# A two-layer graph network on one core: block 0 of x and the line weight loaded as squares of 32 and turned by VectorE

## The chip, the cores and the metric

The kernel runs on one NeuronCore of a Trainium2 chip. The metric is device time in microseconds (us) of one execution: the median of three runs is 1557.29 (1557.27 to 1557.6). Times inside the execution are counted in us from the start of the profiled span.

## The reference

Two layers over 4096 nodes with 512 channels and a dense 4096 x 4096 adjacency of 0 and 1. Cut to what matters:

```python
# layer 0
Ab   = A > 0
keep = Ab & (cumsum(Ab, axis=1) <= 64)            # the first 64 neighbours of each row
cnt  = keep.sum(axis=1, keepdims=True)
xj   = leaky_relu((keep @ X) / max(cnt, 1) @ W_nb.T + b_nb)
xi   = leaky_relu(X @ W_line.T + b_line)
x    = layernorm(X + xi + where(cnt > 0, xj, 0))
# layer 1: attention of one head over the same adjacency
Wh   = x @ W + bW
e    = leaky_relu_0.2((Wh @ a1 + b1)[:, None] + (Wh @ a2 + b2)[None, :])
att  = softmax(where(adj > 0, e, -9e15), axis=1)
x    = layernorm(x + att @ Wh)
```

The change touches the first 25 us of layer 0: the first products `X @ W_nb.T` and `X @ W_line.T`. The kernel takes `X @ W_nb.T` before the sum over neighbours, so that each block of x meets both weights.

## The kernel before, in words

x is cut into 32 blocks of 128 rows. A product on TensorE contracts over the partitions, so a block of x is wanted turned (`xt`, channels on the partitions), and so are both weights (`wt_nb`, `wt_line`). There are two ways to turn a 128 x 512 piece:

- **By TensorE** (`turn_by_pe`, L319): VectorE rearranges the piece into tile `t` (`squares`, L313), TensorE turns four 128 x 128 parts by transposes (L156), and ScalarE (or VectorE, for one piece) copies the bank out of PSUM (L157).
- **By VectorE** (`turn_x`, L332): the piece is loaded by four DMAs of 64 KB, one for each group of 32 partitions, in runs of 512 bytes (`load_turned_x`, L301), so that one VectorE transpose of 32 x 32 squares over the whole tile finishes it.

Before, block 0 (loaded whole into `xb` by `load_own_x`, L308) and all eight pieces of the two weights (`load_w`, L358) go by TensorE; blocks 1 and up go by VectorE, through three buffers `late` (tiles `c`), so that block i + 3 can be loaded once block i is turned.

The order of the work is written out by hand: each engine takes its instructions in the order of the program text, and every engine that issues DMAs (SP, ACT and POOL here) has a queue of its own. A DMA signals its end on one of eight semaphores for the loads of SP and ACT together, and one of another eight for POOL's, taken in turn; an issue that gets a semaphore in use waits for the DMA that holds it.

The start (L438 to L465 of the code) runs so. SP loads block 0, two pieces of nb, block 1 in squares, two pieces of line, and the line bias; ACT loads the other two pieces of nb and two of line. TensorE runs 15 transposes of the identity (`spin`, L364), which warm its clock. Then come the turn of block 0 and of pieces 0 to 2 of nb; the product of block 0 with the first three quarters of nb (L381, width 384), with the turn of piece 3 behind its first matmul; two line pieces; the last quarter (width 128); the other two line pieces; the turn of block 1; block 1 times nb (`pys[1]`), block 0 times line (`pls[0]`). Blocks 2 and 3 are issued on POOL, each behind a small VectorE memset into its buffer (L448), which holds them back until VectorE gets there. The weight of layer 1 (`raw["w"]`), rows of a1, a2 and the bias, and the first two pieces of the adjacency follow on SP behind another memset (L458).

After that come the turn of block 2 (`turn_pair(1, 0)`), differences of the two weights (L517, L518), the two parts of y for blocks 0 and 1 (L431, L432), the turn of block 3 into the buffer that block 0 leaves, the line bias of block 0 (L416), block 1 times line, three sums over blocks 2 and 3 (L502 to L504), and the bias of block 1. ScalarE bends the result (L420) and writes the bias into a bank (L608); then a loop `seven(g)` (products at L511) takes two blocks at a time by a scheme with seven half products in place of eight, and encodes the adjacency beside it.

A line number in the profile is that of the instruction in the source; a helper has one line for all that call it.

Of the kernel before, what the change touches and what calls it, by code (L numbers as in the profile page):

```python
# [9 lines left out]
F32 = mybir.dt.float32  # L10
# [3 lines left out]
I32 = mybir.dt.int32  # L14
# [6 lines left out]
P = 128  # L21
SQ = 32
# [10 lines left out]
def two_layer_adj_gnn(  # L33
# [16 lines left out]
    nc = tc.nc  # L50
    N, C = x.shape
    NB = N // P
    NC = C // P
    NT = NB // 2
    CH = 2048
# [52 lines left out]
    late = [rows.tile([P, C], F32, name="c") for _ in range(3)]  # L108
# [28 lines left out]
    with ExitStack() as l0:  # L137
        adj_p = l0.enter_context(tc.tile_pool(name="l0_adj", bufs=2))
# [10 lines left out]
        def transpose_to(dst, src_of, n, wide, move):  # L149

            if wide:
                pt = ps_acc.tile([P, n, P], F32, name="acc")
            else:
                pt = ps_s.tile([P, n, P], F32, name="pt")
            for k in range(n):
                nc.tensor.transpose(pt[:, k, :], src_of(k), ident)  # L156
            move(dst, pt)  # L157
# [128 lines left out]
        with ExitStack() as la:  # L286
            work = la.enter_context(tc.tile_pool(name="l0_work", bufs=2))
            wp = la.enter_context(tc.tile_pool(name="l0_w", bufs=1))
# [3 lines left out]
            w_t = {}  # L292
            xrs, xbs, xts, pys, pls = {}, {}, {}, {}, {}
            lines = {}

            def load_turned_x(i, queue=nc.gpsimd):

                if i < NB:
                    xrs[i] = late[i % 3].rearrange("p (j c) -> p j c", c=P)
                    for n in range(NC):  # L300
                        queue.dma_start(  # L301
                            xrs[i][ts(n, SQ)],
                            x_blk(i)[:, ts(n, P)].rearrange("(j a) c -> a j c", a=SQ),
                        )

            def load_own_x(i, queue):
                xbs[i] = work.tile([P, C], F32, name="xb", bufs=1)
                queue.dma_start(xbs[i], x_blk(i))  # L308

            def squares(src):  # L310

                t = work.tile([P, C], F32, name="t", bufs=4)
                nc.vector.tensor_copy(  # L313
                    t.rearrange("p (m n b) -> p m n b", m=NC, b=SQ),
                    src.rearrange("p (n m b) -> p m n b", m=NC, b=SQ),
                )
                return t

            def turn_by_pe(dst, src, t=None, wide=False, move=nc.scalar.copy):  # L319
                t = squares(src) if t is None else t  # L320
                transpose_to(dst, lambda m: t[:, ts(m, P)], NC, wide, move)

            def xt_tile():
                return work.tile([P, NC, P], F32, name="xt", bufs=3)

            def turn_x(i, t=None):
                if i < NB:
                    xts[i] = xt_tile() if t is None else t
                    if i == 0:
                        turn_by_pe(xts[i], xbs[i])  # L330
                    else:
                        nc.vector.transpose(  # L332
                            xts[i].rearrange("p m (j a) -> p j m a", a=SQ),
                            xrs.pop(i).rearrange("p j (m b) -> p j m b", b=SQ),
                        )


            def early(name):
                dt = I32 if name == "a" else BF16
                t = adj_p.tile([P, CH], dt, name=name).bitcast(F32)  # L340
                return t.rearrange("p (c q) -> p c q", q=C)

            raw = {}
            for name in ("nb", "line"):
                t = early("a")
                raw[name] = [t[:, c, :] for c in range(NC)]
            raw["w"] = []
            for k in range(2):
                t = early("left")
# [3 lines left out]
            t = early("edge")  # L353
            early_rows += [t[:, c, :] for c in range(NC // 2)]

            def load_w(name, src, queues):
                for c in range(NC):
                    queues[c % len(queues)].dma_start(raw[name][c], src[ts(c, P), :])  # L358

            def spin(n):  # L360

                idle = ps_acc.tile([P, P], F32, name="acc")
                for _ in range(n):
                    nc.tensor.transpose(idle, ident, ident)  # L364

            def turn_w(name, parts=range(NC)):

                if name not in w_t:
                    w_t[name] = wp.tile([P, NC, C], F32, name=f"wt_{name}")
                moved = [squares(raw[name][c]) for c in parts]  # L370
                for c, t in zip(parts, moved):
                    turn_by_pe(
                        w_t[name][:, :, ts(c, P)], None, t, name == "nb",
                        nc.vector.tensor_copy if name == "nb" and c == 1 else nc.scalar.copy,
                    )

            def linear(lhs_t, name, bank=None, part=slice(0, C), behind_first=lambda: None):

                pl = ps_acc.tile([P, C], F32, name="acc") if bank is None else bank
                for k in range(NC):  # L380
                    nc.tensor.matmul(  # L381
                        pl[:, part], lhs_t[:, k, :], w_t[name][:, k, part],
                        start=(k == 0 and part.start == 0),
                        stop=(k == NC - 1 and part.stop == C),
                        skip_group_check=part.stop - part.start < C,
                    )
                    if k == 0:
                        behind_first()
                return pl
# [43 lines left out]
                    y_lo[i], src, y_hi[i].bitcast(F32), ALU.subtract  # L433
                )

            load_own_x(0, nc.sync)
            load_w("nb", w_nb, (nc.scalar, nc.sync))
            load_turned_x(1, nc.sync)  # L438
            load_w("line", w_line, (nc.scalar, nc.sync))
            nc.sync.dma_start(bias_line, b_line.partition_broadcast(P))  # L440
            spin(15)


            turn_x(0)
            turn_w("nb", range(3))

            for i in (2, 3):
                nc.vector.memset(late[i % 3][:, 0:1], 0.0)  # L448
                load_turned_x(i)
            pys[0] = linear(  # L450
                xts[0], "nb", part=slice(0, 3 * P), behind_first=lambda: turn_w("nb", range(3, 4))
            )
            turn_w("line", range(0, 2))
            linear(xts[0], "nb", pys[0], slice(3 * P, C))
            turn_w("line", range(2, 4))
            turn_x(1)
            load_turned_x(4)
            nc.vector.memset(raw["w"][0][:, 0:1], 0.0)  # L458
            load_w("w", w, (nc.sync,))
            load_rows(nc.sync)  # L460
            pys[1] = linear(xts[1], "nb")
            pls[0] = linear(xts.pop(0), "line")

            wide = [pls[0]]

# [29 lines left out]
            def turn_pair(g, r):  # L495
                i = 2 * g + r
                turn_x(i, (top, low)[r](g) if i < EDGE else None)
                load_turned_x(i + 3)
# [111 lines left out]
            for g in range(1, EDGE // 2):  # L610
                steps = idle
                q = done[0]
# [134 lines left out]
        for s in range(NB * NS):  # L747
            i, g = divmod(s, NS)
# [14 lines left out]
            for k in range(KB):  # L763
                j = g * KB + k
# [21 lines left out]
    wp = tile_p("l1_w", 3)  # L786
# [8 lines left out]
    early = wp.tile([P, NI, NS * SQ], F32, name="w")  # L795
# [460 lines left out]
    for q in range(NP * NT):  # L1256
# [6 lines left out]
        b = {2: 2 * g + 3, 3: 2 * g + 4}.get(k, 2 if q == 0 else NB)  # L1263
# [32 lines left out]
    p, rz = banks[NT - 1], rzs[NT - 1]  # L1296
# [62 lines left out]
```

## Time and profile before

| what | us |
|---|---|
| median of three timed runs | 1557.29 |
| lowest, highest | 1557.27, 1557.6 |
| span of the profiled execution, first to last instruction | 1555.1 |
| median less span | 2.19 |
| TensorE busy in the span | 1544.7 |
| TensorE, start of the first product (L381) | 7.79 |
| VectorE, start of the line bias of block 1 (L416) | 24.22 |
| TensorE, start of the product after it (L511) | 26.11 |

The profiled execution shows its span; its time by the device's clock is not listed apart from the three runs, so the span and the median stand side by side.

The profile is read as follows. PE is TensorE, DVE VectorE, ACT ScalarE, POOL GpSimd, SP SyncE; a name with q at its end is that engine's sequencer, which issues DMAs. A line of the timeline has the start, the length, the engine and line, the operation, the tile written and the tile read, the number of instructions merged, and in brackets the idle time before it and what ended it. A line of the waits has who waited, for whom, the total in us, how often, and the longest. A line of the chain has start, length and what the end of the program hung on there.

### The profile page before, as it was taken

What the parts mean: (1) busy time and instruction counts of PE and PEld (TensorE: products, weight loads), DVE (VectorE), ACT (ScalarE), POOL (GpSimd) and SP (SyncE); (2) the same over time, 40 slices, a digit from 0 to 9 for tenths busy, and PEclk for the clock granted to TensorE, in tenths of its full rate; (3) what the DMA queues carried; (4) which work ended last, traced back from release to release, by engine and by line L of the source; (5) the groups of instructions that cost most, each with busy time, mean ns of one, the idle gap of its engine ahead of it and who ended that gap; (6) DMA issues with size and microseconds to landing.
All of it is one profiled execution on the core that took longest, in us unless ns stands there. A gap on an engine that the chain in (4) does not pass through costs nothing.

```text
span 1555.1 us, 19124 instructions
## 1 busy us (share of the span) xinstructions
PE 1544.7 (99%) x6579; PEld 1241.5 (80%) x6579; DVE 1262.8 (81%) x2341; ACT 980.0 (63%) x1183; POOL 267.1 (17%) x424
## 2 busy tenths in 40 slices
PE   9999999999999999999999999999999999999998
PEld 5444468888888888878888888888888888888887
DVE  6988658989999998468888788887888888888864
ACT  3766558887888878427684577555775556755520
POOL 4544212212222122110001001111011110111101
PEclk9999999999999999999999999999999999999999
DMA  8965478879889887654122122221122211222202
GB/s 237 244 203 183 156 206 247 253 241 265 247 220 283 246 254 203 141 133 114 42 60 63 42 42 69 57 66 43 40 69 60 63 47 36 69 64 59 51 4 55
DMA packets 175425, 201.17 MB, mean 129 GB/s; under 512 B 102032, under 2 KB 135568, under 8 KB 167136
## 3 DMA queue, kind: packets, MB, share of 16 engines
q1 hardware_dynamic: 147472, 130.33, 29.7%
q0 software_dynamic: 26224, 67.64, 17.0%
q10 hardware_dynamic: 1632, 1.98, 0.4%
q8 instruction: 51, 0.84, 0.2%
q14 instruction: 46, 0.38, 0.1%
HBM read 141.03 MB, written 42.08 MB: 118 GB/s over the span
## 4 chain that ended last, share of the span: by engine, by line
PE 97%; DVE 1%; DMA 1%; ACT 0%; issue 0%; ACTq 0%; POOLq 0%; DVEq 0%; POOL 0%; SPq 0%
PE acc L1103 35%; PE acc L766 30%; PE pt L1103 14%; PE acc L511 9%; PE acc L917 4%; PE acc L381 3%; DMA w<-x_d 0%; PE pt L381 0%; DMA nat<-code_d 0%; DMA xb<-in_x_dram 0%; PE pt L156 0%; DVE c L849 0%; DMA st_d<-e 0%; PE acc L156 0%; DVE st L117 0%
## 5 line engine op out<-in xcount | busy, mean ns | idle before, releaser
L1103 PE MATMUL acc<-bt,s 128*128 128x256 f32 x1504 | 335.7, 379 | 0.0
L766 PE MATMUL acc<-y_hi,kt 128*128 128x512 f32 x824 | 320.5, 389 | 0.0
L766 PE MATMUL acc<-y_lo,kt 128*128 128x512 f32 x824 | 320.5, 389 | 0.0
L1103 PEld LDWEIGHTS acc<-bt,s 128*128 128x128 f32 x1504 | 285.8, 190 | 38.9
L988 ACT ACTIVATE w<-nat,few 128x1024 f32<-128x1024 uint8 x128 | 137.0, 1136 | 237.9 <-DVE a L1063 237.9
L1103 PE MATMUL acc<-bt,a 128*128 128x256 f32 x1056 | 239.0, 379 | 0.0
L1103 PE MATMUL pt<-bt,a 128*128 128x256 f32 x992 | 224.6, 379 | 0.0
L1103 PEld LDWEIGHTS acc<-bt,a 128*128 128x128 f32 x1056 | 200.6, 190 | 27.3
L1103 PEld LDWEIGHTS pt<-bt,a 128*128 128x128 f32 x992 | 188.5, 190 | 25.6
L280 ACT ACTIVATE kt<-ktb,few 128x1024 fp32r<-128x1024 uint8 x124 | 142.8, 1152 | 97.7 <-PE acc L766 80.1
L1063 DVE STREAM_TRANSPOSE a<-w 128x1024 f32<-128x1024 f32 x128 | 153.1, 1225 | 61.9 <-ACT w L1044 51.0
L126 POOL TENSOR_TENSOR rs<-ve,few 128x1 f32<-128x1 f32 x64 | 46.5, 727 | 807.6 <-DVE ve L124 800.2
L766 PEld LDWEIGHTS acc<-y_lo,kt 128*128 128x128 f32 x824 | 154.7, 188 | 32.2
L766 PEld LDWEIGHTS acc<-y_hi,kt 128*128 128x128 f32 x824 | 154.6, 188 | 32.1
L981 ACT ACTIVATE w<-w,st_n 128x1024 f32<-128x1024 f32 x128 | 149.3, 1232 | 16.1 <-DVE m L998 16.1
L1044 ACT ACTIVATE w<-w,nm 128x1024 f32<-128x1024 f32 x128 | 145.5, 1137 | 11.0 <-DVE nm L1035 11.0
L998 DVE CUSTOM_DVE_ANT_0 w<-e_n,w 128x1024 f32<-128x1024 f32 x128 | 149.5, 1220 | 1.3
L178 ACT ACTIVATE edge<-a,few 128x2048 bf16<-128x2048 int32 x64 | 136.2, 2129 | 4.6 <-issue 2.7
L226 ACT CAST code<-left 128x2048 uint8<-128x2048 bf16 x64 | 121.1, 1893 | 0.0
L209 DVE TENSOR_TENSOR left<-edge,left 128x2048 bf16<-128x2048 bf16 x64 | 78.4, 1225 | 2.2
L301 POOL DMA_DIRECT2D c<-in_x_dram x120 | 65.6, 554 | 64.0 <-DVE xt L332 45.1
L197 DVE TENSOR_TENSOR_SCAN left<-few,ends,left 128x1024 bf16<-128x1024 f32 x32 | 75.2, 2351 | 1.1
(229 smaller groups left out, 1999.4 us busy)
## 6 DMA issues: line engine op xcount, KB each, us to landing
a<-in_adj_dram SPq DMA_DIRECT2D x64, 1024.0 KB, 5.8
code_d<-code POOLq DMA_DIRECT2D x64, 256.0 KB, 4.0
nat<-code_d SPq DMA_DIRECT2D x248, 64.0 KB, 2.2
w<-x_d SPq DMA_DIRECT2D x128, 64.0 KB, 2.1
own<-in_x_dram SPq DMA_DIRECT2D x31, 256.0 KB, 3.2
own<-own_d POOLq DMA_DIRECT2D x31, 256.0 KB, 5.6
x_d<-own POOLq DMA_DIRECT2D x31, 256.0 KB, 4.7
c<-in_x_dram POOLq DMA_DIRECT2D x120, 64.0 KB, 5.0
```

The lines of the kernel that those rows point to most:

```text
L178: nc.scalar.activation(edge_of[s], loaded.pop(s).rearrange("p (t q) -> p q t", q=2), AF.Sigmoid, bias=steep[:, 0:1], scale=STEEP, accum_ou ...
L209: nc.vector.tensor_tensor(left, e, left, ALU.mult)
L226: nc.scalar.copy(code.bitcast(U8).rearrange("p (t q) -> p q t", q=2), seen_of.pop(s))
L280: nc.scalar.activation(kts[s], bytes_.rearrange("p t (i r) -> p t r i", r=2), AF.Sigmoid, bias=steep[:, 1:2], scale=STEEP,)
L511: nc.tensor.matmul(bank, lhs[:, k, :], rhs[:, k, :], start=start and k == 0, stop=k == 1, skip_group_check=True,)
L766: nc.tensor.matmul(accs[i], kt[:, k // 2, k % 2, :], term[j], start=(j == 0 and term is y_hi), stop=(j == NB - 1 and term is y_lo),)
L981: nc.scalar.activation(dst, src, AF.Prelu, bias=bias, scale=scale, alpha=0.2)
L988: nc.scalar.activation(wts[b][:, i, :], nats[b, i // 2].bitcast(U8)[:, i % 2, :], AF.Relu, bias=far, scale=-FAR,)
L998: nc.vector.tensor_tensor_reduce(w_i, e2_n, w_i, 1.0, -3e38, ALU.subtract, ALU.max, m4s[b][:, i : i + 1])
L1044: nc.scalar.activation(w_i, w_i, AF.Exp, bias=nms[b][:, i : i + 1], accum_out=z4s[g][:, r, i : i + 1])
L1063: nc.vector.transpose(a[:, r].rearrange("p s (i a) -> p i s a", a=SQ), wts[2 * g + r][:, :, ts(k, 8 * SQ)].rearrange("p i (s x) -> p i s x ...
L1103: nc.tensor.matmul(banks[g][n], lhs[:, j, :], bt[:, 4 * k + j, rhs, :], start=(k == 0 and j == 0 and n == mate[0]), stop=(k == NP - 1 and ...
```

## The change

Block 0 is loaded like every other block, by four DMAs of squares on SP, and turned by VectorE into `xt`. The line weight is no longer loaded by SP and ACT: sixteen DMAs of squares (four for each of its four pieces) go out on POOL, first of all on that queue, and VectorE turns each piece straight into `wt_line`. Blocks 2 and 3 stand behind these sixteen on POOL, without the memsets. Block 0 times the line weight moves behind block 1 times nb in the text of the program and is cut into quarters, each of four products of width 128, and each right behind the VectorE turn of its piece. The turns of the line pieces thus follow the turn of block 1 on VectorE.

```diff
@@ turn_x
                     xts[i] = xt_tile() if t is None else t
-                    if i == 0:
-                        turn_by_pe(xts[i], xbs[i])
-                    else:
-                        nc.vector.transpose(
-                            xts[i].rearrange("p m (j a) -> p j m a", a=SQ),
-                            xrs.pop(i).rearrange("p j (m b) -> p j m b", b=SQ),
-                        )
+                    nc.vector.transpose(
+                        xts[i].rearrange("p m (j a) -> p j m a", a=SQ),
+                        xrs.pop(i).rearrange("p j (m b) -> p j m b", b=SQ),
+                    )
...
-            for name in ("nb", "line"):
-                t = early("a")
-                raw[name] = [t[:, c, :] for c in range(NC)]
+            t = early("a")
+            raw["nb"] = [t[:, c, :] for c in range(NC)]
+            line_sq = adj_p.tile([P, CH], I32, name="a").bitcast(F32)
+            line_sq = line_sq.rearrange("p (c j q) -> p c j q", c=NC, q=P)
...
+            def load_line(c):
+                for n in range(NC):
+                    nc.gpsimd.dma_start(
+                        line_sq[ts(n, SQ), c],
+                        w_line[ts(c, P), ts(n, P)].rearrange("(j a) c -> a j c", a=SQ),
+                    )
+
+            def turn_line(c):
+                nc.vector.transpose(
+                    w_t["line"][:, :, ts(c, P)].rearrange("p m (j a) -> p j m a", a=SQ),
+                    line_sq[:, c].rearrange("p j (m b) -> p j m b", b=SQ),
+                )
...
-            load_own_x(0, nc.sync)
+            load_turned_x(0, nc.sync)
             load_w("nb", w_nb, (nc.scalar, nc.sync))
+            for c in range(NC):
+                load_line(c)
             load_turned_x(1, nc.sync)
-            load_w("line", w_line, (nc.scalar, nc.sync))
             nc.sync.dma_start(bias_line, b_line.partition_broadcast(P))
             spin(15)
...
+            w_t["line"] = wp.tile([P, NC, C], F32, name="wt_line")
             turn_x(0)
             turn_w("nb", range(3))
-
             for i in (2, 3):
-                nc.vector.memset(late[i % 3][:, 0:1], 0.0)
                 load_turned_x(i)
             pys[0] = linear(
                 xts[0], "nb", part=slice(0, 3 * P), behind_first=lambda: turn_w("nb", range(3, 4))
             )
-            turn_w("line", range(0, 2))
             linear(xts[0], "nb", pys[0], slice(3 * P, C))
-            turn_w("line", range(2, 4))
             turn_x(1)
             load_turned_x(4)
...
             pys[1] = linear(xts[1], "nb")
-            pls[0] = linear(xts.pop(0), "line")
+            pls[0] = None
+            for c in range(NC):
+                turn_line(c)
+                pls[0] = linear(xts[0], "line", pls[0], slice(P * c, P * c + P))
+            xts.pop(0)
```

In the changed text `linear`'s product is at L392, the turn of an x block at L329, the turn of a line piece at L366, its load at L360, and the lines behind the start stand 11 or 12 higher (L416 is L427, L511 is L523).

## Prediction of the time, with its working

> **What bounds the kernel now.** I read four things in order: the shares, TensorE's own waits, the chain that ended last in its first 26 us, and the order of VectorE and GpSimd there. Times are us from the span's start.
>
> The shares and the chain's shares by engine, from the page:
>
> ```profile
> span 1555.1 us, 19124 instructions
> ...
> PE 1544.7 (99%) x6579; PEld 1241.5 (80%) x6579; DVE 1262.8 (81%) x2341; ACT 980.0 (63%) x1183; POOL 267.1 (17%) x424
> ...
> PE 97%; DVE 1%; DMA 1%; ACT 0%; issue 0%; ACTq 0%; POOLq 0%; DVEq 0%; POOL 0%; SPq 0%
> ```
>
> TensorE's waits, all of the run:
>
> ```profile
> PE acc L364 <- POOL ident masks.py:199: 1.4, 1, 1.4
> PE acc L381 <- ACT wt_nb L157: 0.7, 1, 0.7
> PE acc L917 <- DVE acc L929: 0.6, 2, 0.4
> PE acc L511 <- ACT acc L608: 0.2, 1, 0.2
> PE pt L156 <- DVE t L313: 0.2, 1, 0.2
> ```
>
> So nothing later absorbs a shift at the start: between 27 and 420 us TensorE has no wait at all, and what the first stage gains or loses passes to the end one to one. The chain of that stage:
>
> ```profile
> 0.74 3.74 DMA xb<-in_x_dram
> ...
> 7.16 0.59 ACT wt_nb L157
> ...
> 7.79 0.91 PE acc L381 x2
> 8.71 0.44 PE acc L156 x4
> 9.14 1.94 PE acc L381 x6
> 11.08 0.87 PE pt L156 x8
> 11.95 0.89 PE acc L381 x8
> 12.85 0.87 PE pt L156 x8
> 13.72 10.47 PE acc L381 x24
> ...
> 24.22 0.70 DVE t L416
> ```
>
> The first real product starts at 7.79, when the third quarter of nb is turned. From there TensorE is busy to 24.19, and then VectorE's bias addition for block 1 (L416) and two ScalarE steps let it go on at 26.11. The two lines `pt L156 x8` are the sixteen turns of the line weight.
>
> **The change, part by part.** There are two paths to the addition at 24.22, and the later one counts.
>
> *TensorE's path.* Removed behind 7.79: sixteen turns, 0.87 + 0.87 = 1.74. The four turns of block 0 lie before 7.79 and count in the start. Block 0 times the line weight becomes sixteen products of width 128: four such for nb took 0.89, so 3.56, where four of width 512 take 8 × 10.47/24 = 3.49: +0.07. The stretch of 24.19 - 7.79 = 16.40 becomes 14.73. The path is even with before if its first product starts at 24.19 - 14.73 = 9.46; any start before that is gain.
>
> *When does it start?* Block 0 was one transfer on SP at 0.74 that took 3.74. Now four of 64 KB go there, and nb's quarters 1 and 3 queue behind. The squares of block 1 show the price of an issue (min, median, max in ns) and, for all issues of that line up to 14 us, of a landing:
>
> ```profile
> L301 SPq DMA_DIRECT2D c<-in_x_dram x4: 311/371/437, 2.1 to 5.9; - x4
> ...
> DMA to landing us min/median/max: 3.5/4.6/6.3
> ```
>
> With some 0.05 between them, block 0 is issued at 0.74, 1.15, 1.6 and 2.0, nb 1 at 2.4 instead of 1.19. SP's four squares had a median landing of 4.2: block 0 is there at 6.2 (5.5 by the shortest, 8.3 by the longest). Its turn on VectorE is 0.70 (L332), the first nb rearrangement 0.43, which makes 7.3 (6.6 to 9.4). Quarter 1 of nb lands 4.3 to 5.7 after its issue as SP's two did (median 5.0): 7.4 (6.7 to 8.1). From the start of that rearrangement (5.53) to the first product (7.79) were 2.26. So the first product comes at 7.4 + 2.26 = 9.7 (9.0 to 11.7), and TensorE's path is **+0.2** (-0.5 to +2.2). The gain of 1.74 is eaten by nb's later start. Block 1 is needed 4.2 after the first product, at 13.9; SP issues its squares only as earlier loads give their semaphores back (nb 0 landed at 4.6), say by 6.2, so 6.2 + 6.3 + 0.7 = 13.2 at worst: covered.
>
> *VectorE's path.* The line weight moves from SP and ACT (four issues) to GpSimd's queue (sixteen), ahead of blocks 2 and 3. The rows of before:
>
> ```profile
> 7.75 4.56 POOL L301 DMA_DIRECT2D c<-in_x_dram  x8 [6.45 <-DVE c L448]
> ...
> 14.80 0.71 DVE L332 STREAM_TRANSPOSE xt<-c 128x512 f32<-128x512 f32 x1 [1.23 <-DMA c<-in_x_dram]
> ...
> 20.78 0.71 DVE L332 STREAM_TRANSPOSE xt<-c 128x512 f32<-128x512 f32 x1 [1.71 <-PE acc L381]
> ...
> 22.78 0.42 DVE L504 TENSOR_TENSOR lo<-lo,xt 128x256 f32<-128x256 f32 x1
> 24.22 0.69 DVE L416 TENSOR_TENSOR t<-acc,bias_line 128x512 f32<-128x512 f32 x1 [1.02 <-PE acc L381]
> ```
>
> Block 2 was issued at 7.75 and turned at 14.80. From that turn to the end of the three sums (23.20) VectorE needs 8.40 - 1.71 of idling = 6.69, and only then comes the addition of block 1. GpSimd takes 0.55 an issue (median of L301) and is free from 1.31. In the changed order the ninth transfer waits on the semaphore of the first, and each later one on that eight before it. So block 2's fourth square, the twentieth, is the third on its semaphore: issue of the fourth at 1.33 + 3 × 0.55 = 3.0, and then three landings in a row. In before, GpSimd's eight issues from 7.75 on took 5.9 falling to 4.0, and the eight from 14.18 on 4.8 rising to 7.1. I take 5.2, what block 4's took when SP had just begun to load w, as it will here: 3.0 + 15.6 = **18.6**. Then the addition of block 1 can come at 18.6 + 6.69 = 25.3, against 24.22: **+1.1**. With 4.0 each, 15.0, but twenty issues alone and one landing give 1.33 + 19 × 0.55 + 4.0 = 15.8, so 22.5: no delay. With 6.0: 21.0, +3.5. With 7.1, 24.3 and +6.8, an end I count as unlikely, since those shared the engines with 1 MB adjacency loads.
>
> [...]
>
> *What is hidden.* VectorE gains four turns of 0.70 and loses four rearrangements of 0.43 and two memsets; the line turns fall where it idled 1.96, 1.56 and 1.23 in before. The sixteenth line load lands at 5.2 + 2 × 5.2 = 15.6, its turn ends by 16.3, and TensorE wants that quarter at 9.7 + 4.2 + 3.5 + 2.7 = 20.1: 3.8 of cover; if it is gone, each further us is a us. ScalarE's five copies (0.54 to 0.59) and two issues were beside the path. Blocks 4 and 5 follow on GpSimd some 4 us later than before; block 4 lands near 25 and VectorE gets to it at 27.09 + 1.1, block 5 near 29 and is wanted at 29.03 + 1.1. That is the thinnest cover; if gone, VectorE, 97% busy from 30 to 40, has little to give back, so it costs what is missing, some tenths.
>
> **Sum.** The later path rules: +1.1. The span 1555.1 becomes 1556.2. The median of the timed runs, 1557.29, stands 2.19 above the span; with that, **1558.4**.
>
> **The rivals.**
> 1. *A cold TensorE.* The warming transposes end at 4.8, and now the next work comes near 7.3 and the products at 9.7, where before the gaps were 0.16 and 0.68. The start shows two speeds at a granted clock of 1.00:
>
> ```profile
> L364 PE MATMUL acc<-ident x7: 421/421/421, 1.6 to 2.9; 128*128 128x128 f32 x7
> ```
> ```profile
> L156 PE MATMUL acc<-ident,t x4: 272/272/273, 5.6 to 6.0; 128*128 128x128 f32 x4
> ```
> Starts were 0.214 apart in the slow speed (1.63 to 2.7) and 0.109 in the fast, which came after 3.8 of work. Against it: no gap here is long enough to show a falling back. If it does, the products lose half of 3.8, 1.9, and the turns before them 0.4: TensorE's path +2.6 (up to +3.8): 1559.9. [...]
> 2. *GpSimd's queue rules, slower than before.* Landings of 5.9 and more at the crowded start put block 2 at 20.6 or later, from which point the loss is 3.1. At 6.0: +3.5, 1560.8. For it: block 0 and line in 512-byte runs crowd the start; against: the 4.0 seen as the queues ran dry.
> 3. *Early landings.* At 4.0 to 4.8 GpSimd's path vanishes, the first product is at 9.0, and TensorE's path gives -0.5: 1556.8. The floor is a start at 7.79, -1.7.
>
> **How the numbers follow.** Forecast 0.45, cold clock 0.20, GpSimd's queue 0.15, early landings 0.20. A measurement here can tell some 0.2%, 3.1 us, from no change. Slower by that: all of rival 2 and a third of rival 1, 0.22. Faster by that is beyond even the floor: 0.02 for what I overlooked. Within: 0.76. The range leaves out the outer part of rivals 2 and 3 and the worst cold start: 1556.4 to 1561.4.
>
> **What would show it.** Right: the first L392 product near 9.7; block 2's turn near 18.6 and waiting for a DMA; the second bias addition near 25.3, released by VectorE's own order; no sixteen turns. Wrong: narrow products at twice 0.89 per four (cold clock), GpSimd's line loads without waits from the ninth on, or a new TensorE wait behind 30.

## The result, and the profile after

The changed kernel takes 1564.62 us (median of five, 1563.08 to 1567.4); the kernel before took 1557.27 beside it. The ratio is 1.0049, with a 95% interval of 1.0038 to 1.0059: **slower by 7.4 us, some 0.5%**. The forecast was 1558.4 with a range of 1556.4 to 1561.4, so the time lies outside.

The page of the changed kernel, its span, busy shares and chain:

```profile
span 1562.8 us, 19157 instructions
...
PE 1546.6 (99%) x6583; PEld 1243.8 (80%) x6583; DVE 1264.9 (81%) x2339; ACT 977.1 (63%) x1178; POOL 276.3 (18%) x440
...
PE 94%; DMA 2%; DVE 2%; POOL 1%; issue 1%; ACT 0%; ACTq 0%; DVEq 0%; POOLq 0%; SPq 0%
```

TensorE is busy for 1.9 longer although twenty turns have gone: the same work ran slower. Its waits, all of the run (who waited, for whom, total, times, longest):

```profile
PE acc L156 <- DVE t L313: 3.9, 1, 3.9
...
PE acc L523 <- DVE t L587: 0.8, 1, 0.8
PE acc L392 <- ACT wt_nb L157: 0.7, 1, 0.7
...
PE acc L523 <- ACT acc L620: 0.2, 1, 0.2
```

The first line and the second are new. TensorE's order of time shows where they lie:

```profile
1.37 3.26 PE L375 MATMUL acc<-ident 128*128 128x128 f32 x15 [1.37 <-POOL ident masks.py:199]
8.57 2.82 PE L156 MATMUL acc<-ident,t 128*128 128x128 f32 x12 [3.94 <-DVE t L313]
12.06 1.65 PE L392 MATMUL acc<-wt_nb,xt 128*128 128x384 f32 x2 [0.68 <-ACT wt_nb L157]
...
29.41 1.88 PE L523 MATMUL acc<-wt_nb,xt 128*128 128x512 f32 x4
...
46.34 1.98 PE L523 MATMUL acc<-hi,xt 128*128 128x512 f32 x4 [0.79 <-DVE t L587]
```

The first product starts at 12.06 in place of 7.79, the first pair of width 384 takes 1.65 in place of 0.91, and the addition of block 1 comes at 29.61 in place of 24.22. VectorE there:

```profile
7.50 0.71 DVE L329 STREAM_TRANSPOSE xt<-c 128x512 f32<-128x512 f32 x1 [6.50 <-DMA c<-in_x_dram]
...
21.09 0.71 DVE L329 STREAM_TRANSPOSE xt<-c 128x512 f32<-128x512 f32 x1 [4.86 <-DMA c<-in_x_dram]
...
26.18 0.71 DVE L329 STREAM_TRANSPOSE xt<-c 128x512 f32<-128x512 f32 x1 [0.81 <-PE acc L392]
...
28.17 0.42 DVE L516 TENSOR_TENSOR lo<-lo,xt 128x256 f32<-128x256 f32 x1
29.61 0.69 DVE L427 TENSOR_TENSOR t<-acc,bias_line 128x512 f32<-128x512 f32 x1 [1.03 <-PE acc L392]
```

Block 0 is turned at 7.50, block 2 at 21.09 behind 4.86 of waiting for its load. VectorE is through with the sums at 28.59, 1.0 before TensorE lets it go on, and 0.81 of its time before that (at 26.18) was itself a wait for TensorE: from block 2's turn alone it would be 21.09 + 6.69 = 27.8. So **both paths are late**, TensorE's by 5.4 and VectorE's, by itself, by some 3.6.

The sixteen line loads on GpSimd's queue, and the issue of blocks 2 and 3 behind them (the first eight line loads went out in one stretch of 4.56; the ninth, at 6.36, waited 0.26 for a line load to land):

```profile
L360 POOL DMA_DIRECT2D a<-in_L_gnn_W_line_dram x16: 548/556/748, 1.5 to 12.3; - x16
...
DMA to landing us min/median/max: 3.1/5.4/7.1
```
```profile
13.73 4.33 POOL L301 DMA_DIRECT2D c<-in_x_dram  x8 [0.93 <-DMA a<-in_L_gnn_W_line_dram]
```

The windows of the changed kernel (stretch; length; busy time of PE, PEld, DVE, ACT, POOL; granted clock; DMA share; GB/s) say why TensorE is slow:

```profile
5.00:7.00 2.00, 0.00 (x0) 0.00 (x0) 0.00 (x0) 0.00 (x0) 1.64 (x4) 1.00 1.06 235
7.00:9.00 2.00, 0.43 (x2) 0.43 (x3) 1.50 (x4) 0.00 (x0) 1.11 (x2) 0.68 1.09 258
9.00:11.00 2.00, 2.00 (x12) 1.99 (x10) 0.61 (x2) 0.59 (x1) 1.33 (x3) 0.50 1.14 199
...
17.00:19.00 2.00, 2.00 (x12) 1.52 (x11) 0.00 (x0) 0.00 (x0) 1.61 (x3) 0.76 1.08 305
19.00:21.00 2.00, 2.00 (x7) 0.92 (x6) 0.00 (x0) 0.59 (x1) 1.10 (x2) 1.00 0.81 214
```

The clock falls to 0.50 near 7.7 (a mean of 0.68 over the 2 us from 7.00 is full speed for 0.72 us), 3.1 after the last warming transpose ended at 4.63, and is full again near 18.

The loss adds up: 5.39 to the addition of block 1, 0.79 at 46.34, and 1.24 at the very end, which the experiments treat last: 7.4 of the 7.7 by which the span grew.

### The profile page after: what moved, and what is told of

Its sections match the earlier page's. It is cut to its first block, busy times and chain, and to the rows that moved or that the text cites. A ratio compares the mean times of both kernels' runs of the same rounds, so it can differ in the third digit from the quotient of the medians.

```text
span 1562.8 us, 19157 instructions
## 1 busy us (share of the span) xinstructions
PE 1546.6 (99%) x6583; PEld 1243.8 (80%) x6583; DVE 1264.9 (81%) x2339; ACT 977.1 (63%) x1178; POOL 276.3 (18%) x440
## 4 chain that ended last, share of the span: by engine, by line
PE 94%; DMA 2%; DVE 2%; POOL 1%; issue 1%; ACT 0%; ACTq 0%; DVEq 0%; POOLq 0%; SPq 0%
PE acc L1115 35%; PE acc L778 30%; PE pt L1115 14%; PE acc L523 8%; PE acc L929 4%; PE acc L392 2%; DMA c<-in_x_dram 1%; DMA a<-in_L_gnn_W_line_dram 0%; PE pt L392 0%; DMA w<-x_d 0%; POOL a L360 0%; DMA nat<-code_d 0%; POOL c L301 0%; DVE edge L411 0%; DVE c L861 0%
```

## The experiments

Each experiment has one profile, and landings move from profile to profile: block 2 is turned at 21.09 in the changed kernel, and at 21.91 and 23.52 in experiments 1 and 2, whose loads are the same.

**Theories.** A: the clock fell while TensorE waited for block 0, and that is the loss. B: GpSimd's queue, with sixteen line loads ahead of block 2, holds VectorE, and TensorE through it. The two were rivals in the prediction. Times beside before are of the same chip; "the addition" is that of block 1, at 24.22 before.

**1. More warming (spin45).**

```diff
-            spin(15)
+            spin(45)
```

> The changed kernel with 45 warming transposes in place of 15, so that TensorE works until about 8 us. Cold-clock theory (the clock fell back in the 3.9 us of idling before the first turn, and cost 1.0 before the first product and 2.8 behind it): 422 ns transposes become 272, the first product starts near 10.8 in place of 12.06 and the four narrow products of a line quarter keep their 0.89; the time falls. It does not fall by all of that, because block 2 is turned at 21.09 and VectorE needs 6.69 from there: the addition of block 1 comes at 27.8 in place of 29.6, so 1.8 us below the changed kernel, about 1562.8 by the median. GpSimd-queue theory alone (the clock costs nothing that VectorE would not cost): no change from 1564.6.

Measured: 1564.96, ratio 1.0053 (1.0039 to 1.0067), no better than the change. But the profile is another one. The first product moves to 10.97 and runs at full speed (0.91), and TensorE then waits for VectorE (at L620 through ScalarE, which waits for the addition):

```profile
10.97 0.91 PE L392 MATMUL acc<-wt_nb,xt 128*128 128x384 f32 x2 [0.67 <-DVE t L313]
```
```profile
28.42 0.69 DVE L427 TENSOR_TENSOR t<-acc,bias_line 128x512 f32<-128x512 f32 x1
```
```profile
PE acc L523 <- ACT acc L620: 2.1, 1, 2.1
...
PE acc L523 <- DVE t L587: 0.8, 1, 0.8
...
PE acc L523 <- DVE y_lo L443: 0.7, 1, 0.7
PE acc L523 <- DVE acc L605: 0.5, 1, 0.5
```

Block 2 was turned at 21.91 and the addition came at 28.42, only 1.2 earlier. Of that, later waits take most back (0.5 at L605 is new, and those at L929 in the second layer are 0.8 in place of 0.4). The mechanism of A is shown, but its cure alone uncovers B.

**2. No warming (spin1).**

```diff
-            spin(15)
+            spin(1)
```

> The changed kernel with 1 warming transpose in place of 15. Cold-clock theory (TensorE is cold again by the time block 0 has landed, so the warming is lost): the same as the changed kernel, 1564.6. If the warming transposes still help behind the idle time: slower by up to 1 to 2.

Measured: 1564.47, ratio 1.0047 (1.0033 to 1.0060): the same as the change. The first product comes as slow as there, and not later:

```profile
11.81 1.65 PE L392 MATMUL acc<-wt_nb,xt 128*128 128x384 f32 x2 [0.67 <-ACT wt_nb L157]
```

So in the changed kernel the fifteen transposes do nothing for the first products any more. That the times agree is in part chance: here the addition, at 30.03, was held by VectorE (block 2 was turned at 23.52), while TensorE's path was through 1.2 earlier than in the changed kernel.

**3. Block 0 alone (x0_only).** The kernel before, with only block 0 as squares:

```diff
... (turn_x as in the change)
-            load_own_x(0, nc.sync)
+            load_turned_x(0, nc.sync)
```

> Only the first half of the change: block 0 comes as squares on SP and is turned by VectorE, the line weight is loaded and turned as before. Cold-clock theory: the first product near 12, with slow products until about 18 and the sixteen line turns among them; addition of block 1 near 30 to 31, so +6 to +7 against before, about 1564: this half alone makes the whole loss. GpSimd-queue theory: block 2 is early again, so the loss nearly vanishes: 1558.

Measured: 1562.26 against 1556.91, ratio 1.0036 (1.0023 to 1.0049). The first product is slow, and the addition 5.3 late, with no wait for VectorE:

```profile
11.28 1.65 PE L378 MATMUL acc<-wt_nb,xt 128*128 128x384 f32 x2 [0.68 <-ACT wt_nb L157]
```
```profile
29.52 0.69 DVE L413 TENSOR_TENSOR t<-acc,bias_line 128x512 f32<-128x512 f32 x1 [1.02 <-PE acc L378]
```

The half of the change that concerns block 0 costs 5.3 by itself: the late start and the cold clock together.

**4. Block 0 alone, with more warming (x0_only_spin45).** Both edits of 3 and 1.

> Block 0 as squares, the line weight as before, and 45 warming transposes in place of 15. Here block 2 is early (turned at 15.06 in the run of block 0 alone), so TensorE's path rules by itself. Cold-clock theory: fast turns and products, first product near 10.3 in place of 11.28, addition of block 1 at 10.3 + 16.4 = 26.7 in place of 29.5; about 2.8 below the kernel with block 0 alone, so 1559.5. If the squares of block 0 cost only by landing late and the clock is no matter: no change from 1562.3.

Measured: 1560.75 against 1557.06, ratio 1.0024 (1.0015 to 1.0034). The profile of this kernel, TensorE and then VectorE:

```profile
10.89 0.91 PE L378 MATMUL acc<-wt_nb,xt 128*128 128x384 f32 x2 [0.68 <-DVE t L313]
```
```profile
27.16 0.69 DVE L413 TENSOR_TENSOR t<-acc,bias_line 128x512 f32<-128x512 f32 x1 [1.02 <-PE acc L378]
```

The addition is 2.36 earlier than in 3, which is the price of the cold clock where nothing else is in the way; it is nearer 2.95 for a like start, since block 0 was turned 0.59 later here (7.61 against 7.02). The time fell by less than the 2.8 expected (1.7 on the differences to before), since the waits at L914 in the second layer grew from one of 0.4 to two of 1.6 together; why, I did not follow. The other 2.9 (some 2.4 for the like start) are the late start.

**5. The line weight alone (line_only).** The changed kernel, with block 0 whole and turned by TensorE as before:

```diff
... (turn_x as in the kernel before)
-            load_turned_x(0, nc.sync)
+            load_own_x(0, nc.sync)
```

> Only the second half of the change: block 0 comes whole and is turned by TensorE as before, the line weight comes as squares on GpSimd and is multiplied in quarters. Cold-clock theory: the first product is back near 7.8 to 8.5, the clock stays fast, and TensorE's path alone would bring a gain of about 1; VectorE's path (block 2 behind sixteen line loads, turned near 20.5) rules and makes about +3 against before: 1560. If the squares of block 0 were not the trouble: no better than the changed kernel.

Measured: 1562.98 against 1556.91, ratio 1.0041 (1.0029 to 1.0054): twice the loss expected. TensorE's first product starts at 7.96, at full speed (0.91), and then it waits (first its waits, then VectorE):

```profile
PE acc L526 <- DVE y_lo L446: 3.6, 1, 3.6
```
```profile
18.04 0.71 DVE L369 STREAM_TRANSPOSE wt_line<-a 128x512 f32<-128x512 f32 x1 [4.17 <-DMA a<-in_L_gnn_W_line_dram]
22.71 0.71 DVE L332 STREAM_TRANSPOSE xt<-c 128x512 f32<-128x512 f32 x1 [3.96 <-DMA c<-in_x_dram]
```

The addition comes at 29.22, +5.0. So the half of the line weight costs about as much by itself as the half of block 0. They don't add (the addition is 5.3 and 5.0 late with one half, 5.4 with both), since the later path counts; curing one helps little while the other stands. The wait of 3.6 here also let the clock fall to 0.50 from about 25.7 to 32.5.

**6. Block 2 first on GpSimd (spin45_x2first).** With the longer warming:

```diff
-            spin(15)
+            spin(45)
...
+            load_turned_x(2)
             for c in range(NC):
                 load_line(c)
...
-            for i in (2, 3):
-                load_turned_x(i)
+            load_turned_x(3)
```

> The changed kernel with 45 warming transposes and with block 2 issued on GpSimd ahead of the sixteen line loads (block 3 stays behind them). With both theories true: the first product near 10.8, block 2 is turned right behind the line pieces at about 17 to 18, and VectorE no longer rules; the addition of block 1 at 10.8 + 14.73 = 25.5, +1.3 against before, about 1558.6. If only the cold clock matters: the same as the long warming alone. If block 3, now last on the queue, takes the place of block 2: about as the long warming alone, with VectorE waiting for a DMA at the turn of block 3.

Measured: 1564.90, ratio 1.0053 (1.0041 to 1.0066). Missed: neither block 3 nor block 2 ruled, but the last line piece, turned at 21.32 in place of 15.69, and VectorE's order put the addition at 28.43 as in 1. In the changed kernel block 2 had the seventeenth to twentieth place on GpSimd's queue, here the last line piece has it: block 2 was turned at 21.09 there, that piece at 21.32 here.

**7. The same bytes in four transfers on GpSimd (line4_gpsimd).** Experiment 5 with

```diff
...
-            def load_line(c):
-                for n in range(NC):
-                    nc.gpsimd.dma_start(
-                        line_sq[ts(n, SQ), c],
-                        w_line[ts(c, P), ts(n, P)].rearrange("(j a) c -> a j c", a=SQ),
-                    )
+            def load_line(n, queue):
+                queue.dma_start(
+                    line_sq[ts(n, SQ)].rearrange("p c j q -> p (c j) q"),
+                    w_line[:, ts(n, P)].rearrange("(j a) c -> a j c", a=SQ),
+                )
```

> As the kernel with the second half of the change alone (block 0 whole, line squares on GpSimd ahead of blocks 2 and 3), but the line weight comes in four transfers of 256 KB instead of sixteen of 64 KB: the same bytes in the same 512-byte runs on the same queue, with four semaphores instead of sixteen. If the eight semaphores hold the queue: block 2's issue no longer waits for any line transfer, it is turned at 15 to 17 in place of 22.71 and the addition of block 1 comes near 23, about 1556 to 1557 in place of 1562.98. If the bytes themselves on that queue, or the crowd at the start, are what costs: block 2 still near 20 or later and the time near 1561.

Measured: 1563.11, ratio 1.0042 (1.0030 to 1.0055). Four line loads and the four of block 2 went out on GpSimd without a wait, and the ninth issue waited 2.08 for a line load. Block 2 was there in time, turned at 18.17 with no wait. But now block 1, on SP's queue, is late, and TensorE waited 3.5 for it:

```profile
15.12 0.71 DVE L332 STREAM_TRANSPOSE xt<-c 128x512 f32<-128x512 f32 x1 [6.90 <-DMA c<-in_x_dram]
```

Behind this wait TensorE was slow too: the eight products of block 1 took 5.37, where they took 3.60 in x0_only_spin45. Four transfers in place of sixteen thus moved the wait from block 2 to block 1 and left the time as it was. Do the transfer engines fall behind? The windows of before, and of the changed kernel, over the same stretch:

```profile
5.00:8.00 3.00, 2.32 (x17) 2.09 (x18) 2.37 (x8) 1.66 (x3) 0.24 (x1) 1.00 1.07 362
```
```profile
5.00:8.00 3.00, 0.00 (x0) 0.00 (x0) 0.51 (x1) 0.00 (x0) 2.19 (x5) 0.95 1.06 268
```

The sixteen engines are full in both (share 1.07 and 1.06), but move 362 GB/s before and 268 after. From 2 to 14 us it is 278 against 239, 3.34 MB against 2.86. What lowers the rate is not shown. The squares come in runs of 512 bytes, but over these 3 us x0_only, with block 0 in squares, moves 348, hold_line (run 11), with no line load until 7.1, only 256, and no run changes the length of the runs alone. Experiment 8 shows that the lower rate by itself does not make the loss.

**8. The line weight in four transfers on ACT and SP, block 0 whole (line4_x0whole).** The loading function of 7, with block 1 ahead of it and blocks 2 and 3 held by their memsets as before:

```diff
             load_turned_x(1, nc.sync)
+            for n in range(NC):
+                load_line(n, nc.scalar if n == 0 else nc.sync)
```

> Block 0 whole as before; the line weight as squares, but in four transfers of 256 KB on the queues of ACT (one) and SP (three) instead of sixteen on GpSimd; blocks 2 and 3 on GpSimd as before. Both theories: no cold clock (first product near 7.8) and no long queue in front of block 2 (turned near 15); the sixteen line turns are gone from TensorE, so the addition of block 1 comes at 7.8 + 14.7 = 22.5 to 23, -1.2 to -1.7 against before: 1555.7, faster than both. If turning the line weight by VectorE is itself the trouble: slower than before.

Measured: 1556.19 against 1557.06, ratio 0.9997 (0.9988 to 1.0006): not to be told from before. First product at 8.25, at full speed (0.91), the addition at 23.46, 0.8 earlier than in before's profile. VectorE has the rest: it waits 3.76 for the line weight and then has no idle time.

```profile
14.58 2.49 DVE L368 STREAM_TRANSPOSE wt_line<-a 128x512 f32<-128x512 f32 x4 [3.76 <-DMA a<-in_L_gnn_W_line_dram]
16.99 0.67 DVE L332 STREAM_TRANSPOSE xt<-c 128x512 f32<-128x512 f32 x1
...
23.46 0.68 DVE L429 TENSOR_TENSOR t<-acc,bias_line 128x512 f32<-128x512 f32 x1
```

So turning line by VectorE is not the trouble; when its bytes, and those of the blocks, arrive is. Nor is the rate of the engines: it is as low as in the changed kernel, over 5 to 8 us and from 2 to 14 (244 GB/s against 239).

```profile
5.00:8.00 3.00, 2.19 (x16) 1.72 (x16) 1.94 (x8) 1.46 (x3) 0.00 (x0) 1.00 1.16 267
```

Against experiment 7 three things differ at once, the queue of the line weight, its place behind block 1, and the memsets ahead of blocks 2 and 3; which of them counts is not told apart.

**9. The turn of block 2 ahead of the line turns (line4_x2early).** On 8:

```diff
+            top1 = xt_tile()
+            turn_x(2, top1)
+            load_turned_x(5)
+            y_terms(0, pys[0])()
             pls[0] = None
             for c in range(NC):
                 turn_line(c)
...
-            turn_pair(1, 0)
...
-            for i in range(2):
-                y_terms(i, pys[i])()
+            y_terms(1, pys[1])()
```

> The kernel with block 0 whole and the line weight in four transfers on ACT and SP, and on VectorE the turn of block 2 and the low part of y of block 0 ahead of the four line turns, where it idled 3.8 us for the line weight. There the addition of block 1 came at 23.46, held by VectorE, and TensorE could have gone on at 22.9. If VectorE's order is what is left: 22.9, some 0.5 earlier, about 1555.7; TensorE is then the bound. If the line weight lands later still: no change from 1556.2.

Measured: 1558.72, ratio 1.0012 (1.0004 to 1.0021): a miss, slower than before (and than 8, where the intervals just touch). Block 2 landed later than the line weight, and the line turns now stood behind it:

```profile
16.45 0.71 DVE L332 STREAM_TRANSPOSE xt<-c 128x512 f32<-128x512 f32 x1 [5.66 <-DMA c<-in_x_dram]
```

TensorE waited 2.1 for the first line piece.

**10. Both cures on the change itself (line4_spin45).** The changed kernel with 45 transposes and the loads of 8; block 0 still in squares.

> The changed kernel with both cures: 45 warming transposes, and the line weight in four transfers on ACT and SP. Block 0 still comes as squares. Both theories: first product near 10.6, addition of block 1 at 25.3, no later wait; +1.1 to +1.5 against before, 1558.4, which is near what was forecast for the change itself. If a third cause remains: near 1562.

Measured: 1560.55 against 1557.06, ratio 1.0023 (1.0014 to 1.0032). The first product comes at 11.29 at full speed (0.91), the addition at 26.77, +2.55; the wait of 0.8 at L587 is still there, the tail is not. Less than the change costs by about half, more than expected by 2.1: block 0, turned only at 8.01, and block 2 at 20.26.

**11. The line loads held back (hold_line).** The changed kernel, with

```diff
             turn_x(0)
+            nc.vector.memset(line_sq[:, :, 0, 0:1], 0.0)
+            for c in range(NC):
+                load_line(c)
```

in place of the loads at the start.

> The changed kernel with its sixteen GpSimd line loads held back by a small VectorE memset until block 0 has been turned. It asks why block 0's squares landed at 7.5 and not at the 6.2 that was forecast. If the crowd from GpSimd makes it: block 0 is turned near 6.2 and the first product comes 1.3 earlier, near 10.8. If the 512-byte runs beside the nb loads make it by themselves: still 7.0 to 7.5. Either way the line weight and block 2 come 6 us later than in the changed kernel, so the time is above it: 1567 to 1570.

Measured: 1569.73, ratio 1.0085 (1.0071 to 1.0099), as late as expected. The question it asked has a clear answer:

```profile
6.40 0.71 DVE L329 STREAM_TRANSPOSE xt<-c 128x512 f32<-128x512 f32 x1 [5.41 <-DMA c<-in_x_dram]
```

With no line load beside it block 0 is turned at 6.40, 1.1 earlier. GpSimd's queue is not needed for a late landing: where block 0 came as squares and the line weight on SP and ACT, it was turned at 7.02 (x0_only), 7.61 (x0_only_spin45) and 8.01 (line4_spin45).

The run shows a second thing. TensorE idled only 2.69 before its first turn, and the clock fell all the same, at about 8.7 (a mean of 0.62 from 8 to 11):

```profile
7.52 1.72 PE L156 MATMUL acc<-ident,t 128*128 128x128 f32 x12 [2.69 <-DVE t L313]
9.92 1.65 PE L392 MATMUL acc<-wt_nb,xt 128*128 128x384 f32 x2 [0.68 <-ACT wt_nb L157]
```
```profile
8.00:11.00 3.00, 2.32 (x12) 1.58 (x11) 1.80 (x5) 1.17 (x2) 3.00 (x6) 0.62 0.56 175
```

**12. The tail (pool_extra).** The kernel before, with sixteen more GpSimd transfers of 3 KB to scratch memory in the middle of the second layer:

```diff
+        if q == 30:
+            for d in extra_d:
+                nc.gpsimd.dma_start(d, few)
```

> The kernel before with sixteen more small GpSimd transfers (3 KB each, of a constant, into scratch memory nobody reads) in the middle of the second layer. It asks about the tail: in the profiles with sixteen more GpSimd transfers the span ends 5.7 us after the last SP issue, in all others 4.4. If the number of GpSimd transfers makes the tail: 5.7 here too, and the time about 1.3 above before. If not: 4.4, and no change in time.

Measured: 1558.06 against 1556.72, ratio 1.0009 (1.0000 to 1.0018), +1.3, which by the times alone just touches no change. The last SP issue of the kernels before, after and pool_extra:

```profile
1550.67 0.34 SPq L1324 DMA_DIRECT2D out_dram<-c  x1
```
```profile
1557.13 0.34 SPq L1336 DMA_DIRECT2D out_dram<-c  x1
```
```profile
1551.07 0.34 SPq L1328 DMA_DIRECT2D out_dram<-c  x1
```

Their spans are 1555.1, 1562.8 and 1556.8, so 4.43, 5.67 and 5.73 remain behind that issue. In the kernels without more GpSimd transfers than before it is 4.4 (x0_only, x0_only_spin45, line4_x0whole, line4_spin45, line4_x2early), with sixteen more 5.7 (after, spin1, spin45, line_only, spin45_x2first, hold_line), with four large ones 5.5. In before, after, x0_only and line_only that last SP transfer landed 1.8 to 1.9 after its issue. Nothing is on record in the rest of the tail, so what runs there stays open; that more GpSimd transfers, at the start or half-way, make it longer is shown.

## Why the prediction was wrong, point by point

- **TensorE's stretch** was sized rightly for a full clock. From the first product to the end of block 1 times line it was to be 14.73: 10.97 to about 25.5 in spin45, 8.25 to about 22.8 in line4_x0whole. The 1.74 of turns went, the quarters cost next to nothing.
- **Rival 1, the cold clock: given 0.20, it happened.** The sum took TensorE's path at full speed, +0.2; it measured +5.4. I wrote that no gap was long enough to show a falling back. That was the step that failed, for the trace of before does show it, in a place I did not look: its end. Windows of before:

```profile
1550.00:1551.00 1.00, 0.00 (x0) 0.00 (x0) 0.73 (x2) 0.00 (x0) 0.20 (x1) 1.00 0.30 111
1551.00:1552.00 1.00, 0.00 (x0) 0.00 (x0) 0.00 (x0) 0.00 (x0) 0.00 (x0) 0.81 0.88 303
1552.00:1553.00 1.00, 0.00 (x0) 0.00 (x0) 0.00 (x0) 0.00 (x0) 0.00 (x0) 0.50 0.33 111
```

  The last product ends at 1547.7 and the clock falls at about 1551.6, after 3.9 of idling. My forecast had TensorE without work from 4.8 to 7.3 and with little until 9.7; with block 0 at 7.5 the gap became 3.94. The late landing is not all of it: 2.69 were enough in hold_line, so the 2.5 of my own forecast were at risk, though no run has just that gap. In line_only the clock fell 2.3 after the last product (23.39 to 25.68). Transposes alone were enough to hold the speed: behind the 45 of spin45, which ran from 1.37 to 8.62, the twelve turns took 1.53 in place of 2.82 and the first pair of products 0.91.
- **Its price** was too low as well: 1.9 for the products and 0.4 for the turns forecast, 2.8 (17.52 against 14.73) and about 1.3 measured, because the clock stayed low from 7.7 to 18, not for 3.8 of work. Uncovered, in runs 3 and 4, the difference at the addition was 2.36, or 2.95 for a like start.
- **Block 0's landing**: 6.2 forecast, 7.5 measured. The start time of the first product, 9.7, became 12.06: some 1.1 from here and 1.3 from the slow turns. With no line load beside it the landing was 6.4; I priced block 0 from transfers that had less beside them.
- **VectorE's path, and rival 2**: block 2 at 18.6 forecast, 21.09 measured. Three landings of 5.2 was too low: the line loads took a median of 5.4, up to 7.1, and block 2's last square was issued at 15.4 instead of 13.4 and took another 5.7. 21.0 was the case of 6.0 each, which I gave 0.15. For block 2 it came true, though in the changed kernel's profile TensorE's path was the later one.
- **That the later path counts** was right, and is why no single cure helped much. But I gave A and B chances as alternatives, and they came together. That both come from one thing, a start with more short runs than the engines pass, is not shown: x0_only has A with 348 GB/s, and line4_x0whole has neither at 267.
- **The thinnest cover**, block 5: wanted near 30 by the forecast, it was turned at 35.34 behind 0.83 of waiting, and TensorE paid 0.79 at 46.34. "Some tenths" was the right size.
- **The tail** of 1.24 was in no term of the sum.
- **The last words of the forecast** held in two points: block 2's turn waited for a DMA (4.86), and there is a new TensorE wait behind 30 (0.79). The products of width 128 were not slow: they took 275 ns each, as in before, for the first of them started at 18.08, with the clock full again; slow were the eight of width 384, 847 ns in the median against 486 in before. Of the line loads behind the eighth, only four waited visibly, 2.1 in all.

The first forecast of what the loss is made of thus fails in sizes on both paths, and by the tail. What stays open: what runs in the tail, why two waits in the second layer grew where the start was earlier, and what makes the same line weight cost on GpSimd's queue and nothing behind block 1 on ACT and SP.

## What to carry to other kernels

Before a start is made to wait longer, look for the place in the trace where the clock falls, the end of the span included, and price the wait twice: as the wait, and as the slow work behind it; here a wait of 2.7 us was enough. Where many loads start together, the place of each can count more than the rate: here the same line weight in the same short runs cost some 6 us on GpSimd's queue and nothing behind block 1 on ACT and SP, with the engines as full and as slow (268 and 267 GB/s from 5 to 8 us). Where two paths end within two microseconds of each other, undo both in one run, for either alone will look innocent.

## What the runs showed of the hardware that was not expected

- The granted clock reads 1.00 from the start of the span, though the first transposes ran at the slow 421 ns; and it reads 1.00 in the windows of spin1 from 7 to 21 us, where the first pair of products took 1.65. In the changed kernel reading and speed agree from the first change on: at 0.50 a product of width 384 took 847 ns in the median, against 486 in before, and at 1.00, from 18.08, one of width 128 took 275 as in before.
- The fallen clock stayed low for 10.24 in the changed kernel (7.70 to 17.94) and for 6.83 in x0_only (8.49 to 15.32) and in line_only (25.68 to 32.5), which are three and two times 3.41. In line4_gpsimd the products of block 1 lost 1.77 behind the wait, which at half speed makes an estimate of 3.5, once that step, though TensorE worked through all of it.
- In the 3.41 us before each of five falls TensorE had been busy for 0 to 1.2: 0.3 in the changed kernel, 0.4 in x0_only, 1.1 in line_only, 1.2 in hold_line near 8.7, and 0 at the end of before. Gaps of 2.1, in spin45 and line4_x2early, left it 1.3 and did not slow the products behind them. So a gap need not be as long as the step; how short it can be is not shown.
- More GpSimd transfers made the end of the program 1.1 to 1.3 us longer, and that with four of 256 KB, sixteen of 64 KB, or sixteen of 3 KB half-way through.
- Engines at a full share move very different amounts, and the loss does not follow them. From 5 to 8 us, at shares of 1.06 to 1.16, it was 362 GB/s before, 348 in x0_only (slower by 5.4), 268 in the changed kernel (by 7.4) and 267 in line4_x0whole (no slower).
